# A graph network in one kernel: the third layer's early products run in an even line, their sums stay in the PSUM bank, and ten row slots are kept

## The chip, the cores and the metric

The kernel runs on one core of one Trainium2 chip. The metric is the device time of one execution, in microseconds (us). The kernel before took 2517.03 us (median of three runs, 2515.44 to 2526.33). One further execution was profiled and took 2523.93 us.

## What is computed

A layer norm with ReLU, four graph layers on 6250 nodes and 100000 edges (sorted by destination), a last linear map, and a residual. Cut to what matters:

```python
h = relu(layernorm(x))                                        # 6250 x 256
h = h @ W1_self + mean(h[src] by dst) @ W1_neigh + b1         # layer 1
hp = relu(h @ W2_pool + b2_pool)
h = h @ W2_self + max(hp[src] by dst) @ W2_neigh + b2         # layer 2: max pooling
h = ((sum(h[src] by dst) + h) / (deg + 1)) @ W3_neigh + b3    # layer 3: a sum by dst
h = h @ W4_self + mean(h[src] by dst) @ W4_neigh + b4         # layer 4
return x + h @ W_fc + b_fc
```

## The kernel before, in words

Nodes stand in 49 tiles of 128, and destinations are unevenly spread: the first 23 tiles hold most edges. For these, the sum over edges is a dense product: 128x128 blocks of edge counts (`tab_a`, fp8, built in layers 1 and 2) times the rows of the source tiles. For the other tiles it is done edge by edge.

Only layer 2 and what is run inside it matter here. **The chain of layer 2** is the loop over `at`, 1 to 782. In each turn GpSimd (POOL) gathers 128 rows of 2 KB for 128 edges (L1803) into one half of a row pair `X`, of which six are in flight, and VectorE (DVE) takes running maxima (L1784): three steps for two gathers. SyncE's queue (SP) stores one row of each pair (L1788). POOL can fill a pair again only when DVE and the store are through with it. The edges are cut into six blocks, worked last block first; at a block's end `carry` joins the lanes (PE transposes, L1524, then DVE scans, L1537).

**Node tiles.** When a block is done, the node tiles that end in it can be finished by `done2`, a generator that takes one step for each turn: POOL gathers the totals (`tot`, L1658), PE transposes them and multiplies (`pm_prf`, L1689 to L1695), ScalarE (ACT) takes the high part (L1702), PE subtracts it (L1708), ACT takes the low part (L1711), stores both on its own queue (L1712, L1713) and looks at their size (L1597). At most one tile is begun each 11 turns, and not while a block's end is open; beyond that a straight pace holds: `begun2 < 49 * (at - 112) / 634`.

**Early products.** Layer 3 needs, for each of the 23 dense destination tiles, a sum over all source tiles. For source tiles 8 to 39 this is done inside layer 2, as soon as four tiles are finished (a batch of 4): 23 products of 4 items, 92 items, and 736 items in all eight batches. One item is a pair of matmuls (`dense`: L626 with the low fp16 part, L631 with the high part), 512 columns each. A product accumulates in one of two PSUM banks `pd`. SP loads its edge counts (`ae`, L1752, 14 buffers), ACT widens them to fp32 (`aw`, L1739, 4 buffers). After a product, its sum goes into `acc3[d]` in SBUF (printed as `acc`): the first time by an ACT copy (L1438), after that by a DVE add that reads the bank (L1435, `add3`). The call stands with the last but one item of the next product. From `at` 321 on, each turn issues `ceil(left / 48)` items, `left` being what has been added and not issued.

The rows of finished tiles lie in 11 slots (`row_parts`): 8 in `kept_rows`, 3 in a pool of their own.

**Prologue.** Before layer 1, 17 groups of node tiles are normed. `steps` makes products of weights (`pt_w` L285, `pm_w` L291, put away by ACT at L298), one step a group from group 3 and two in groups 7 to 12. They need `w2pf`, loaded by POOL (L1100). In the same turns PE transposes the edge keys (`pt_e`, L1015) and finds where each row of keys begins (`pa`, L932, L934).

Instructions stand on each engine in the order that a scheduler makes of this code; each engine runs its own in that order.

Of the kernel before, what the change touches and what calls it, by code (L numbers as in the profile page):

```python
# [21 lines left out]
P = 128  # L22
# [67 lines left out]
def fast_path(  # L90
# [164 lines left out]
    at = 0  # L255
# [355 lines left out]
                pass  # L611
        del todo[:]

    def dense(ss, block, rows, F, psd, done, extra=0, wide=False, own=None):

        hold = {}

        def run(s):
            if s == ss[0]:
                hold[0] = bank(psd, "pd", "pd", (2 * F if wide else F + extra,))  # L620
            a = block(s)
            z = rows(s)
            if wide:
                nc.tensor.matmul(hold[0], a[0], z, start=(s == ss[0]), stop=(s == ss[-1]))  # L624
            else:
                nc.tensor.matmul(hold[0][:, : F + extra], a[1], z[1][:, : F + extra],  # L626
                                 start=(s == ss[0]), stop=False)
                if s == own:
                    nc.tensor.matmul(hold[0], ident_b, z[1], start=False, stop=False)
                    nc.tensor.matmul(hold[0], ident_r, z[0], start=False, stop=False)  # L630
                nc.tensor.matmul(hold[0][:, :F], a[0], z[0], start=False, stop=(s == ss[-1]))  # L631
            if s == ss[-1]:
                done(hold[0])

        return [lambda s=s: run(s) for s in ss]
# [129 lines left out]
    with ExitStack() as pro:  # L765
# [666 lines left out]
    def add3(d, v):  # L1432

        if d in begun:
            nc.vector.tensor_add(acc3[d], acc3[d], v)  # L1435
        else:
            begun.add(d)
            nc.scalar.copy(acc3[d], v)  # L1438
# [7 lines left out]
    with tc.tile_pool(name="fl2c", bufs=1) as ck, ExitStack() as late:  # L1446
# [273 lines left out]


        BATCH = 4
        ROWS3 = 2 * BATCH + 3
        ready = []
        early = Hub()
        early_pool, split_pool = [], []
        over = {}
        summed = []

        def take_sums():  # L1730
            while summed:
                add3(*summed.pop(0))

        loaded = []

# [5 lines left out]
        def early_products():  # L1741
            batch = dict(ready)
            ss = sorted(batch)
            ready.clear()
            over.update({s: len(early.work) + H3 * len(ss) for s in ss})
            for d in range(H3):
                got = {}
                loaded.append(got)

                def load(d=d, got=got, i=len(loaded) - 1):  # L1750
                    got[0] = early_pool[0].tile([P, BATCH, P], F8, name="ae", bufs=14)
                    nc.sync.dma_start(got[0][:, : len(ss), :].bitcast(BF16),  # L1752
                                      tab_a[d, :, ss[0] : ss[-1] + 1, :])
                    if i >= 2:
                        widened(loaded[i - 2])

                def rows_at(s, got=got):
                    widened(got)
                    return got[1][:, s - ss[0], :], got[0][:, s - ss[0], :]

                work = dense(ss, rows_at, lambda s: batch[s], FH, psd,
                             lambda v, d=d: summed.append((d, v)), own=d)
# [32 lines left out]
        for b in reversed(range(NB)):  # L1795
# [3 lines left out]
            for s0 in range(0, tb, G2):  # L1799
                X = (xmore if at // G2 % 2 else xpool).tile([P, G2, FH], F32, name="X2")  # L1800
                for k in range(G2):
# [27 lines left out]
                    if at == MADE_AT:  # L1829
                        for _ in steps:  # L1830
                            pass
                        top.close()
                        kept_rows += [span3.tile([P, KEPT, FH], dt, tag=f"kept{i}",
                                                 name=f"kept_rows{i}", bufs=1)
                                      for i, dt in enumerate((F32R, F16))]
                        split_pool.append(
# [100 lines left out]
    with ExitStack() as on:  # L1937
# [44 lines left out]
        with tc.tile_pool(name="fl3", bufs=2) as wk:  # L1982
# [37 lines left out]
                yield 1  # L2020

            late = ((0, 4), (4, KEPT), (EARLY[1], 45), (45, NT))
            Z3 = {s: (kept_rows[0][:, s, :], kept_rows[1][:, s, :]) for s in range(KEPT)}
# [694 lines left out]
```

## Time and profile before

| | |
|---|---|
| median of three runs | 2517.03 us |
| the profiled execution | 2523.93 us, its span 2522.0 us |
| busy: PE, DVE, ACT, POOL | 86%, 80%, 50%, 69% of the span |
| layer 2's gathers | from about 650 to 1806 us |
| the early items | from 1125 us on, 624 begun by 1600 us, 112 after |

The page gives busy time by engine; views of the trace give it by stretch, by group of instructions and by instruction, with what ended the idle time before one (`<-`). A busy PE is not a PE at its peak, since matmuls overlap: the distance between two starts is what one costs. PEclk is the clock that PE was granted, as a share of full speed.

### The profile page before, as it was taken

The page shows a single profiled execution, that of the slowest core. Times are in us where ns is not written, and L with a number is a line of the kernel's source. Part 1 is how long each engine was busy: PE and PEld are TensorE (multiplying, and loading weights), DVE is VectorE, ACT ScalarE, POOL GpSimd, SP SyncE. Part 2 cuts the span into 40 slices and gives each one's busy share as a digit, 9 for nine tenths or more (in the row PEclk, how much of TensorE's full clock was granted, in tenths as well). Part 3 has the DMA queues.
Part 4 walks back from the last instruction along what each step waited for, and adds up shares of the span by engine and source line. Part 5 has one row for each costly group of instructions (what it writes and reads, how often), then busy time and mean ns, then how long its engine had stood idle before and what let it go on. Part 6 is the DMA issues. An engine that isn't in the chain of part 4 may idle for free.

```text
span 2522.0 us, 35297 instructions
## 1 busy us (share of the span) xinstructions
PE 2158.2 (86%) x9402; PEld 1248.5 (50%) x9402; DVE 2010.3 (80%) x5565; ACT 1273.2 (50%) x2569; POOL 1729.6 (69%) x2013
## 2 busy tenths in 40 slices
PE   4699999999795565769999999896389999799997
PEld 2456666776443232334444444343244444477776
DVE  7899987785799898888889999798757777467665
ACT  4888888676488787765323333231112222244443
POOL 5477776667566777676667665677477777477775
PEclk9799999999897787789999999898799999899999
DMA  9677777777899999999999999999799999899997
GB/s 306 198 231 233 223 210 213 216 235 238 294 364 303 341 350 346 323 367 357 334 307 339 342 335 301 299 361 326 258 395 407 407 407 407 319 359 333 335 310 234
DMA packets 381357, 785.68 MB, mean 312 GB/s; under 512 B 56430, under 2 KB 175830, under 8 KB 381116
## 3 DMA queue, kind: packets, MB, share of 16 engines
q0 software_dynamic: 135184, 471.64, 56.0%
q1 hardware_dynamic: 158504, 221.70, 24.4%
q10 hardware_dynamic: 87460, 90.01, 10.7%
q8 instruction: 76, 1.25, 0.2%
q14 instruction: 133, 1.09, 0.1%
HBM read 573.99 MB, written 209.94 MB: 311 GB/s over the span
## 4 chain that ended last, share of the span: by engine, by line
PE 45%; DMA 27%; DVE 14%; issue 5%; ACT 5%; POOL 4%; ACTq 0%; DVEq 0%; POOLq 0%; SPq 0%
DMA X<-rows,srcIf 9%; PE pd L626 8%; PE pd L631 8%; PE pd L624 6%; DMA xq<-acc 5%; PE pm_prf L1695 3%; DVE run L1784 3%; DMA ring<-tab_s,srcE 3%; PE pm_hp L1271 3%; PE pm_prf L1689 2%; DMA rows<-X 2%; PE pm_hp L1265 2%; POOL X L1803 2%; PE pm_prf L1692 2%; PE pg L568 2%
## 5 line engine op out<-in xcount | busy, mean ns | idle before, releaser
L1803 POOL DMA_INDIRECT X<-rows,srcIf x782 | 742.7, 950 | 346.1 <-issue 148.8
L1784 DVE SCALAR_TENSOR_TENSOR run<-run,samef,X 128x512 f32<-128x512 f32 x758 | 572.9, 756 | 31.8 <-DMA X<-rows,srcIf 27.0
L548 POOL DMA_INDIRECT ring<-tab_h,srcT x402 | 389.6, 969 | 177.6 <-issue 39.9
L1912 ACT CAST af<-ac 128x640 fp32r<-128x640 fp8e4 (+2 forms) x299 | 217.2, 734 | 339.3 <-PE pd L624 121.7
L548 POOL DMA_INDIRECT ring<-tab_r,srcE x254 | 255.0, 1004 | 102.8 <-issue 35.1
L1784 DVE SCALAR_TENSOR_TENSOR X<-X,samef,run 128x512 f32<-128x512 f32 x379 | 281.9, 744 | 40.2 <-issue 19.7
L548 POOL DMA_INDIRECT ring<-tab_s,srcE x254 | 244.5, 963 | 93.0 <-issue 23.5
L602 DVE SCALAR_TENSOR_TENSOR acc<-pg,M,acc 128x256 f32<-128x256 f32 (+2 forms) x556 | 281.3, 533 | 31.6 <-PE pg L573 16.3
L573 PE MATMUL pg<-ring,hot 128*128 128x256 f32 (+1 forms) x656 | 292.2, 455 | 0.0
L631 PE MATMUL pd<-kept_rows,aw 128*128 128x512 f32 x529 | 271.0, 588 | 0.0
L1739 ACT CAST aw<-ae 128x512 fp32r<-128x512 fp8e4 x184 | 113.8, 620 | 252.1 <-PE pd L631 225.0
L570 PE MATMUL pg<-ring,hot 128*128 128x259 f16 (+1 forms) x656 | 211.5, 325 | 28.7 <-DMA ring<-tab_r,srcE 8.3
L626 PE MATMUL pd<-kept_rows,ae 128*128 128x512 f16 x529 | 208.5, 394 | 10.7 <-DMA ae<-tab_a 8.4
L1695 PE MATMUL pm_prf<-unf,hTf 128*128 128x512 f32 x384 | 196.9, 637 | 6.1 <-ACT hTf L1685 5.4
L631 PE MATMUL pd<-Z1h,af 128*128 128x256 f32 x588 | 194.8, 364 | 1.0 <-ACT af L1299 1.0
L544 DVE TENSOR_SCALAR hot<-iota_bf,keyE 128x128 fp32r<-128x128 bf16 x508 | 138.3, 300 | 48.2 <-PE pg L573 22.7
L624 PE MATMUL pd<-zt,af 128*128 128x512 f32 x598 | 166.3, 398 | 1.5 <-ACT af L1912 1.5
L626 PEld LDWEIGHTS <-ae 128*128 128x128 fp8e4 x736 | 71.3, 97 | 193.0 <-issue 176.6
L626 PE MATMUL pd<-Z1l,A 128*128 128x259 f16 x588 | 158.5, 280 | 0.0
L573 PEld LDWEIGHTS pg<-ring,hot 128*128 128x128 f32 x656 | 130.7, 199 | 47.7 <-issue 39.1
L624 PE MATMUL pd<-z,af 128*128 128x512 f32 x529 | 149.1, 400 | 2.8 <-ACT af L1912 1.5
L463 ACT ACTIVATE A<-pb 128x392 fp8e4<-128x392 f32 x240 | 116.2, 495 | 69.7 <-PE pb L457 65.7
(439 smaller groups left out, 5027.7 us busy)
## 6 DMA issues: line engine op xcount, KB each, us to landing
rows<-X SPq DMA_DIRECT2D x385, 256.0 KB
rows<-hpf SPq DMA_DIRECT2D x49, 256.0 KB
th<-tab_t ACTq DMA_DIRECT2D x49, 256.0 KB
X<-rows,srcIf POOLq DMA_INDIRECT x782
ae<-tab_a SPq DMA_DIRECT2D x184, 64.0 KB
tab_a<-A ACTq DMA_DIRECT2D x15, 784.0 KB
ac<-tab_a ACTq DMA_DIRECT2D x138, 80.0 KB
tab_t<-th SPq DMA_DIRECT2D x37, 256.0 KB
```

The lines of the kernel that those rows point to most:

```text
L544: nc.vector.tensor_scalar(hot[j], iota_b, keyT[:, j - jb : j - jb + 1], None, op0=ALU.is_equal)
L548: nc.gpsimd.indirect_dma_start(out=ring[:, j % deep, :].bitcast(F32), out_offset=None, in_=table, in_offset=bass.IndirectOffsetOnAxis(ap=s ...
L570: nc.tensor.matmul(pg[:, : F + counts], hot[j].bitcast(BF16)[:, 1::2], X.bitcast(F16)[:, 2 * F : 3 * F + counts], start=(k == 0), stop=False)
L573: mm = nc.tensor.matmul(pg[:, :F], hot[j], X[:, :F], start=False, stop=(k == n - 1))
L602: nc.vector.scalar_tensor_tensor(acc[d], half, m, acc[d], op0=ALU.mult, op1=ALU.add)
L624: nc.tensor.matmul(hold[0], a[0], z, start=(s == ss[0]), stop=(s == ss[-1]))
L626: nc.tensor.matmul(hold[0][:, : F + extra], a[1], z[1][:, : F + extra], start=(s == ss[0]), stop=False)
L631: nc.tensor.matmul(hold[0][:, :F], a[0], z[0], start=False, stop=(s == ss[-1]))
L1695: nc.tensor.matmul(pm, hT[:, c, :], un[:, c, :], start=False, stop=(c == KH - 1))
L1784: nc.vector.scalar_tensor_tensor(put, held, st, row, op0=ALU.mult, op1=ALU.max)
L1803: nc.gpsimd.indirect_dma_start(out=X[:, k, :], out_offset=None, in_=tab_p, in_offset=bass.IndirectOffsetOnAxis(ap=srcI[:, t : t + 1], axis=0),
L1912: nc.scalar.copy(wide[i][:, :n, :], got[i][:, :n, :])
```

## The change

1. The sums stay in PSUM. Before a product that continues a sum, ACT copies `acc3[d]` into the product's bank (`lay`, one product ahead), all its matmuls accumulate onto that, and ACT copies the bank back (`take_sums`). The 161 DVE adds are gone; ACT has 161 copies out and 161 copies in that it did not have. Out and in now stand with the second item of a product.
2. The early items run in a line: by turn `at`, `736 * (at - 320) / 432` items have been issued, as far as they exist.
3. The tiles' pace has four corners: 0 at turn 112, 19 at 318, 37 at 612, 49 at 746.
4. 13 slots for rows, 10 of them in `kept_rows`. A row that takes a slot first issues what is left of the products that read the slot's last row.
5. The prologue's product steps begin at group 4, and groups 7 to 13 take two.

```diff
-FIRST_AT = 112
 EARLY_AT = 310
+SLOTS = (10, 13)
+PACE = ((112, 0), (318, 19), (612, 37), (746, 49))
...
             if s == ss[0]:
-                hold[0] = bank(psd, "pd", "pd", (2 * F if wide else F + extra,))
+                hold[1] = True
+                if begun:
+                    hold[0], hold[1] = begun()
+                else:
+                    hold[0] = bank(psd, "pd", "pd", (2 * F if wide else F + extra,))
...
-                                 start=(s == ss[0]), stop=False)
+                                 start=(s == ss[0] and hold[1]), stop=False, **more)
...
-                for _ in range(2 if 7 <= g < 13 else g >= 3):
+                for _ in range(2 if 7 <= g < 14 else g >= 4):
                     next(steps, None)
...
         def row_parts(d):
-            i = d % ROWS3
-            assert early.done >= over.get(d + ROWS3, 0)
+            i = slot[d]
+            if d in held_by:
+                early.advance(over[held_by[d]])
...
-            if i < KEPT:
+            if i < SLOTS[0]:
...
+        early_all = H3 * (EARLY[1] - EARLY[0])
...
         def take_sums():
             while summed:
-                add3(*summed.pop(0))
+                d, v = summed.pop(0)
+                begun.add(d)
+                nc.scalar.copy(acc3[d], v)
+
+        def lay(i):
+            if i < len(order3) and i not in laid:
+                t = bank(psd, "pd", "pd")
+                d = order3[i]
+                laid[i] = t, d not in begun
+                if d in begun:
+                    nc.scalar.copy(t, acc3[d])
...
-                def then(w):
+                def then(w, i=i):
                     take_sums()
+                    lay(i + 1)
                     w()
 
-                early.add([(load, work[0])] + [lambda w=w, i=i: then(w) if i == len(work) - 2 else w()
-                                               for i, w in enumerate(work[1:])])
+                early.add([(load, work[0]), lambda w=work[1], then=then: then(w), *work[2:]])
...
+        def paced(at):
+            for (a0, n0), (a1, n1) in zip(PACE, PACE[1:]):
+                if at < a1:
+                    break
+            return n0 + (n1 - n0) * (at - a0) / (a1 - a0)
...
-                        early.advance(early.done + math.ceil(
-                            early.left() / max(1, min(48, T - 24 - at))))
+                        early.advance(math.ceil(early_all * (at - EARLY_AT - 10)
+                                                / (T - 40 - EARLY_AT)))
...
-                            and begun2 < NT * (at - FIRST_AT) / (T - 36 - FIRST_AT)):
+                            and begun2 < paced(at)):
```

What moves is shown at three places; line numbers after the change are a few higher. First DVE, in the third batch of early products, before. `X` is a row pair (the number is its buffer), `run` the running maximum, `acc_1` the sum of destination tile 1, `pd` the bank:

```order
L1784 SCALAR_TENSOR_TENSOR run<-run,samef,X_16590 128x512
L1435 TENSOR_TENSOR acc_1_10192<-acc_1_10192,pd 128x512
L1784 SCALAR_TENSOR_TENSOR X_16590<-X_16590,samef,run 128x512
L1784 SCALAR_TENSOR_TENSOR run<-run,samef,X_16590 128x512
L1784 SCALAR_TENSOR_TENSOR run<-run,samef,X_16619 128x512
L1784 SCALAR_TENSOR_TENSOR X_16619<-X_16619,samef,run 128x512
L1784 SCALAR_TENSOR_TENSOR run<-run,samef,X_16619 128x512
L1784 SCALAR_TENSOR_TENSOR run<-run,samef,X_16649 128x512
L1435 TENSOR_TENSOR acc_2_10193<-acc_2_10193,pd 128x512
```

And DVE in the same part of layer 2 now:

```order
L1820 SCALAR_TENSOR_TENSOR run<-run,samef,X_16802 128x512
L1820 SCALAR_TENSOR_TENSOR X_16802<-X_16802,samef,run 128x512
L1820 SCALAR_TENSOR_TENSOR run<-run,samef,X_16802 128x512
L1820 SCALAR_TENSOR_TENSOR run<-run,samef,X_16827 128x512
L1820 SCALAR_TENSOR_TENSOR X_16827<-X_16827,samef,run 128x512
```

Only the running maxima are left on DVE there. Second ACT, in the second batch, before: `aw` is the widened count block, `kept_rows`, `hTf`, `th` and `tab_r` belong to node tiles:

```order
L1685 COPY hTf<-pt_hTf 128x512
L1739 CAST aw<-ae 128x512 x2
L1664 DMA th_15666<-tab_t 128x512
L1739 CAST aw<-ae 128x512
L1702 CAST kept_rows_11380<-pm_prf 128x512
L1712 DMA tab_r<-kept_rows_11380 128x512
L1597 ACTIVATE hTf,zsum<-kept_rows_11380 128x512
L1739 CAST aw<-ae 128x512 x3
```

And now:

```order
L1753 COPY acc_8_10199<-pd 128x512
L1768 CAST aw<-ae 128x512
L1761 COPY pd<-acc_10_10201 128x512
L1710 CAST kept_rows_11380<-pm_prf 128x512
L1720 DMA tab_r<-kept_rows_11380 128x512
L1605 ACTIVATE hTf,zsum<-kept_rows_11380 128x512
L1753 COPY acc_9_10200<-pd 128x512
L1768 CAST aw<-ae 128x512
L1761 COPY pd<-acc_11_10202 128x512
```

For each product ACT empties the last bank (L1753), widens a block, and fills the same bank for the product after the next (L1761); a node tile's copies stand between. Third PE in the prologue, before:

```order
L1015 MATMUL pt_e<-identf,rF 128x128 x5
L285 MATMUL pt_w<-identf,wl 128x128 x4
L291 MATMUL pm_w<-w2pf,wT 128x512 x4
L1015 MATMUL pt_e<-identf,rF 128x128 x5
L932 MATMUL pa<-SN,sel_261 128x2
```

And now:

```order
L1022 MATMUL pt_e<-identf,rF 128x128 x5
L939 MATMUL pa<-SN,sel_261 128x2
L941 LDWEIGHTS later
L941 MATMUL pa<-unit,later 128x2
L939 MATMUL pa<-SN,sel_261 128x2
L941 LDWEIGHTS later
L941 MATMUL pa<-unit,later 128x2
L939 MATMUL pa<-SN,sel_261 128x2
L1022 MATMUL pt_e<-identf,rF 128x128 x5
L286 MATMUL pt_w<-identf,wl 128x128 x4
L292 MATMUL pm_w<-w2pf,wT 128x512 x2
```

The second set of key transposes and the first row starts now stand ahead of the first product with the loaded weights `w2pf`.

More of the change, by code (lines that the diff above doesn't have):

```diff
@@ L612, in sums, with dense @@
         del todo[:]
-    def dense(ss, block, rows, F, psd, done, extra=0, wide=False, own=None):
+    def dense(ss, block, rows, F, psd, done, extra=0, wide=False, own=None, begun=None):
         hold = {}
@@ L625, in run @@
             else:
+                more = {} if hold[1] else {"skip_group_check": True}
                 nc.tensor.matmul(hold[0][:, : F + extra], a[1], z[1][:, : F + extra],
-                                 start=(s == ss[0]), stop=False)
+                                 start=(s == ss[0] and hold[1]), stop=False, **more)
                 if s == own:
-                    nc.tensor.matmul(hold[0], ident_b, z[1], start=False, stop=False)
-                    nc.tensor.matmul(hold[0], ident_r, z[0], start=False, stop=False)
-                nc.tensor.matmul(hold[0][:, :F], a[0], z[0], start=False, stop=(s == ss[-1]))
+                    nc.tensor.matmul(hold[0], ident_b, z[1], start=False, stop=False, **more)
+                    nc.tensor.matmul(hold[0], ident_r, z[0], start=False, stop=False, **more)
+                nc.tensor.matmul(hold[0][:, :F], a[0], z[0], start=False, stop=(s == ss[-1]),
+                                 **more)
             if s == ss[-1]:
@@ L1722, in fast_path @@
         BATCH = 4
-        ROWS3 = 2 * BATCH + 3
+        slot, held_by, last = {}, {}, {}
+        for d in reversed(range(NT)):
+            slot[d] = i = (EARLY[1] - 1 - d) % SLOTS[1] if d >= 4 else 3 - d
+            assert d >= KEPT or i < SLOTS[0]
+            if d < EARLY[1]:
+                if i in last:
+                    held_by[d] = last[i]
+                last[i] = d
+        assert all(d >= EARLY[0] for d in held_by.values())
+        early_all = H3 * (EARLY[1] - EARLY[0])
         ready = []
@@ L1759, in rows_at, with begin @@
                     return got[1][:, s - ss[0], :], got[0][:, s - ss[0], :]
+                i = len(order3)
+                order3.append(d)
+                def begin(i=i):
+                    lay(i)
+                    return laid.pop(i)
                 work = dense(ss, rows_at, lambda s: batch[s], FH, psd,
-                             lambda v, d=d: summed.append((d, v)), own=d)
-                def then(w):
+                             lambda v, d=d: summed.append((d, v)), own=d, begun=begin)
+                def then(w, i=i):
                     take_sums()
+                    lay(i + 1)
                     w()
-                early.add([(load, work[0])] + [lambda w=w, i=i: then(w) if i == len(work) - 2 else w()
-                                               for i, w in enumerate(work[1:])])
+                early.add([(load, work[0]), lambda w=work[1], then=then: then(w), *work[2:]])
         todo = []
@@ L1832, in fast_path @@
                         top.close()
-                        kept_rows += [span3.tile([P, KEPT, FH], dt, tag=f"kept{i}",
+                        kept_rows += [span3.tile([P, SLOTS[0], FH], dt, tag=f"kept{i}",
                                                  name=f"kept_rows{i}", bufs=1)
@@ L2022, in fast_path @@
             late = ((0, 4), (4, KEPT), (EARLY[1], 45), (45, NT))
-            Z3 = {s: (kept_rows[0][:, s, :], kept_rows[1][:, s, :]) for s in range(KEPT)}
+            Z3 = {s: tuple(v[:, slot[s], :] for v in kept_rows) for s in range(KEPT)}
             with tc.issue_after(kept_stores[-1].ins):
```

1 line of the change is left out of this document (added).

## The prediction

> **What bounds the kernel now.** I read the page first, then the table of windows for the stretch in which early products run, then the groups and the waits of its slowest part, then single instructions. POOL leads the chain of layer 2: its last gather is what layer 3 waits for. So the question in each window is how many gathers POOL gets through (its columns come last before PEclk), and who holds it.
>
> ```profile
> span 2522.0 us, 35297 instructions
> core 0: us, PE busy (x) PEld busy (x) DVE busy (x) ACT busy (x) POOL busy (x), PEclk, DMA share, GB/s
> 1103.00:1200.00 97.00, 82.38 (x287) 38.18 (x287) 81.03 (x180) 45.76 (x85) 69.55 (x75) 0.93 1.02 367
> 1200.00:1600.00 400.00, 393.81 (x1476) 191.57 (x1474) 363.81 (x546) 122.41 (x222) 265.42 (x280) 0.99 0.96 324
> 1103.00:1600.00 497.00, 476.18 (x1761) 229.75 (x1761) 444.85 (x725) 168.18 (x306) 334.97 (x354) 0.98 0.97 333
> 1125.00:1600.00 475.00, 458.83 (x1716) 221.57 (x1716) 427.01 (x686) 157.50 (x289) 318.36 (x336) 0.98 0.97 329
> 1600.00:1700.00 100.00, 87.31 (x294) 42.41 (x294) 80.72 (x122) 26.74 (x53) 72.99 (x78) 0.93 0.97 339
> 1600.00:1725.00 125.00, 103.93 (x364) 49.74 (x364) 104.33 (x157) 30.82 (x59) 89.51 (x96) 0.93 0.95 328
> 1725.00:1806.00 81.00, 35.77 (x95) 17.72 (x95) 67.04 (x103) 9.23 (x20) 57.74 (x61) 0.71 0.97 331
> ```
>
> One POOL instruction takes 97 / 75 = 1.29 us from 1103 to 1200, 400 / 280 = 1.43 from 1200 to 1600, and 100 / 78 = 1.28 after that. The slow stretch is where DVE adds sums. Undisturbed, POOL issues one each 1.25 us, 0.95 busy and 0.30 of issue:
>
> ```profile
> 1401.35 0.94 POOL L1803 DMA_INDIRECT X<-rows,srcIf  x1 [0.30 <-issue]
> 1405.10 0.95 POOL L1803 DMA_INDIRECT X<-rows,srcIf  x1 [0.30 <-issue]
> L1803 POOL DMA_INDIRECT X<-rows,srcIf x262 | 248.6, 949 | 127.4 <-issue 49.9 <-DVE run L1784 42.0 <-DVE X L1784 13.5
> L1784 DVE SCALAR_TENSOR_TENSOR run<-run,samef,X 128x512 f32<-128x512 f32 x256 | 193.3, 755 | 3.7 <-DMA X<-rows,srcIf 1.0
> L1784 DVE SCALAR_TENSOR_TENSOR X<-X,samef,run 128x512 f32<-128x512 f32 x128 | 95.3, 745 | 5.2 <-issue 1.6 <-DMA X<-rows,srcIf 1.1
> L1435 DVE TENSOR_TENSOR acc<-acc,pd 128x512 f32<-128x512 f32 x129 | 88.3, 685 | 20.4 <-PE pd L631 18.1 <-ACT kept_rows L1702 0.9
> ```
>
> The first two lines are single gathers (start, duration), the others the groups from 1200 to 1600. DVE is the holder: POOL waits for its steps, and DVE waits for a gathered row only 1.0 + 1.1 us in 400. It is busy 363.81 us, of which the adds are 88.3, and idle 20.4 before the adds: 384 of 400. But PE is busy 393.81 of the same 400. Two bounds lie on each other, and the change takes away one of them.
>
> **The change part by part.** The sum is made against the profiled execution, 2523.93 us (span 2522.0 and 1.9 around it), which is 6.9 above the median of 2517.03; the difference found is then taken from the median.
>
> *The adds leave DVE.* From 1200 to 1600, 88.3 + 20.4 = 109 us go from DVE, which then needs 364 - 88 = 276 of 400. Late next is POOL itself. From 1103 to 1600 it has 354 instructions: 354 x 1.25 = 442 us at its own pace, 354 x 1.29 = 457 at the pace it has on either side. I take 1.29, since carries at block ends and waits for stores stay: 497 - 457 = **-40 us**. The lower end is 442 (-55).
>
> *Can PE follow?* From 1125, where early items begin, PE is busy 458.8 us. One item is one pair, 0.46 us:
>
> ```profile
> 1407.86 0.39 PE L626 MATMUL pd<-kept_rows,ae 128*128 128x512 f16 x1
> 1408.32 0.39 PE L626 MATMUL pd<-kept_rows,ae 128*128 128x512 f16 x1
> 1100.00:1600.00 500.00, 244.63 (x624) 60.34 (x624) 0.98 0.97 333
> 1600.00:1806.00 206.00, 44.47 (x112) 11.01 (x112) 0.85 0.96 329
> 1403.37 1.88 PE L1695 MATMUL pm_prf<-unf,hTf 128*128 128x512 f32 x4
> ```
>
> (The third and fourth lines count items, the fifth is a quarter of a node tile's products: next start 1.72 later, so 7 us a tile, about 8 with transposes.) The old rule, worked through the loop, has issued 607 items by gather 643, the last one before 1600; the line 736 x 323 / 432 = 550. That is 57 x 0.46 = 26 us less. The new pace, with its 11 turns between tiles and block ends, has begun 17 tiles by turn 320 and not 16: 8 us less. PE needs 459 - 26 - 8 = 425 us, and has 457 - 22 (from 1103 to 1125) = 435. It fits, with 10 us to spare. The tile that comes earlier lies where PE has room, 37 busy of 50, so it costs nothing there:
>
> ```profile
> 1050.00:1100.00 50.00, 37.42 (x116) 16.82 (x117) 43.63 (x112) 40.56 (x97) 36.04 (x39) 0.86 0.98 344
> ```
>
> If that room were gone, it would cost its 8 us.
>
> *Fills and empties on ACT.* ACT was busy 122 of 400 us. It gets about 114 products' copies out and in before 1600 (550 / 4 less the first 23). No row shows ACT writing a bank from SBUF; the nearest are a bank read to SBUF and an SBUF pass:
>
> ```profile
> L1438 ACT COPY acc<-pd 128x512 f32<-128x512 f32 x23 | 13.5, 586 | 21.5 <-PE pd L631 21.4
> L1597 ACT ACTIVATE hTf<-r2h 128x512 f32<-128x512 f32 x9 | 5.7, 630 | 1.4 <-DMA ae<-tab_a 1.0 <-ACT r2h L1702 0.4
> L1739 ACT CAST aw<-ae 128x512 fp32r<-128x512 fp8e4 x131 | 81.1, 619 | 195.9 <-PE pd L631 175.6 <-DMA rows<-X 10.1 <-DMA ae<-tab_a 5.0
> ```
>
> I take 0.6 us. ACT's 114 x 1.2 = 137 us fit beside its 122. What is new is a chain: a bank's last matmul, copy out 0.59, a widening 0.62 that stands between, copy in 0.6, then the first matmul of the product after the next. That is 1.8 us and the hand-overs, and PE meanwhile has one product, 4 x 0.46 = 1.84. Where products follow back to back, PE waits 0 to 0.3 us each; where a node tile's matmuls lie between, nothing. Queued behind a late copy are the node tiles' copies on ACT, and PE waits for those too. Half of 0.3 for 114 products is 17 us, 10 of which are PE's room: **+8 us** (0 to +35, the upper end with 0.4 us at each). What longer waits do shows in one place, where PE once waited for a late add:
>
> ```profile
> 1198.43 0.38 PE L626 MATMUL pd<-r2l,ae 128*128 128x512 f16 x1 [2.73 <-DVE acc L1435]
> 1199.57 0.60 PE L626 MATMUL pd<-kept_rows,ae 128*128 128x512 f16 x1
> 1200.39 0.65 PE L626 MATMUL pd<-kept_rows,ae 128*128 128x512 f16 x1
> ```
>
> After 2.73 us of waiting, pairs are 0.82 apart instead of 0.46. The row shows it for a wait of that length alone, and I expect shorter ones. The Trainium skill (TensorE: Matmul & The Clock Gate, A second HAM failure mode: psum-queue depth-cycling) says that short idle times between groups of matmuls that cycle through PSUM banks are enough to swing the clock between half and full. By that rule the sum would be the second rival's below. PEclk of 0.98 from 1125 to 1600, with products cycling through two banks, does not bear it out so far.
>
> *The end of layer 2.* The line has 186 items left at gather 643, not 129: 26 us more for PE after 1600. There PE idles 125 - 104 = 21 us up to 1725 and 45 after. But node tiles come at their densest, and a carry makes DVE wait for PE's transposes. I charge half: **+13 us** (0 to +26).
>
> *The prologue.* PE's queue stood still for a load, with the key transposes behind it:
>
> ```profile
> 33.47 6.46 PE L291 MATMUL pm_w<-w2pf,wT 128*128 128x512 f32 x8 [11.01 <-DMA w2pf<-in_L_gnn_W_pool]
> 40.40 0.89 DVE L1019 CAST srcT<-pt_e 128x512 int32<-128x512 f32 x2 [3.16 <-PE pt_e L1015]
> 39.96 0.60 ACT L298 ACTIVATE Wa<-pm_w 128x512 f32<-128x512 f32 x1 [11.47 <-PE pm_w L291]
> 34.75 0.43 DVE L808 BATCH_NORM_STATS2 st<-xt 128x6 f32<-128x256 f32 x1 [5.05 <-DMA xt<-in_x]
> ```
>
> The transposes now go first, and DVE's 3.16 us go: **-3 us** (-6 to +1; DVE's other wait, for `xt`, stays, and the products end a group later).
>
> *The slots* add no instruction. A tile that takes a slot 13 tiles on finds its products issued: tile 26 takes tile 39's at about turn 383, when the line stands at 107 and the batch ends at 92. Cost nothing; a burst of items on PE if the line lagged.
>
> Sum: -40 + 8 + 13 - 3 = **-22 us**, 2501.9 for the profiled execution and **2495** for the median.
>
> **The rivals.**
> *PE stays the bound.* If each fill costs 0.4 us, PE needs 425 + 46 = 471 us from 1125, and the stretch 493 instead of 497. With +5 to +13 at the end and -3: 2517 - 4 + 9 - 3 = 2519. For it: PE at 393.81 of 400. Against: 34 us of its work go elsewhere.
> *Waits for fills lower PE's clock (slower).* Place: the first matmul of each continued product. At a PEclk of 0.86, as in the row of 1050 to 1100, 425 us become 494, the stretch 516: +19, +13 at the end, -3: 2546. It decides for slower once the mean clock there falls below 425 / 475 = 0.89. Against: PE is given work without gaps. The skill's rule above speaks for it.
> *Transfers set the pace.* DMA share is 0.96 where gathers are slow. Then the stretch gains some 8 us and the rest adds up to 2517. Against: 367 GB/s at 1.29 us a gather, and DVE that waits for rows 2 us in 400.
> *Nothing holds POOL any more.* 1.25 us throughout, fills hidden, no charge at the end: 2517 - 55 - 4 = 2458.
> *The change doesn't even anything out.* The order of the program shows the adds gone and the copies there, so only the line's effect could be missing; that is the first rival.
>
> **How the numbers follow.** The forecast gets 0.50, POOL alone 0.10, PE as bound 0.20, transfers 0.08, the lower clock 0.12. A difference of 0.5% is 12.6 us, about what a measurement of this kernel can tell from no change. The forecast with its own uncertainty (-22, its terms -55 to +1 at their ends) is mostly beyond that: faster 0.48 + 0.10 = 0.58; same 0.02 + 0.20 + 0.08 = 0.30; slower 0.12. The range, 2466 to 2526, leaves out the lower clock and half of the lowest case.
>
> **What would show it.** Right: from the first early item on, POOL at 1.28 to 1.31 us an instruction, waiting for `issue` and not for DVE; DVE 75 to 80% busy; 345 ACT copies between `acc` and `pd` (184 out, 161 in) at 0.6; PE waiting for ACT at `pd` under 20 us in sum and PEclk at 0.97 or more; the last gather some 20 us earlier; layer 1's first gather 3 us earlier. Wrong: PE waiting for the copy in at most products, PEclk under 0.9, or POOL still at 1.4 with DVE idle.

## The result, and the profile after

The changed kernel takes 2510.06 us (median of six runs, 2508.67 to 2512.47); the kernel before, in six runs beside them, 2525.15 us (2515.44 to 2528.47). The ratio is 0.9948, 95% interval 0.9931 to 0.9965: faster by 13 us, where 22 were forecast (the medians lie 15 us apart, and the six runs of the kernel before spread over 13). The profiled execution took 2510.62 us, its span 2508.7.

First the table of windows of the changed kernel, for the stretch and for the end of layer 2 (columns as before: PE, PEld, DVE, ACT, POOL with instructions, then PEclk, DMA share, GB/s):

```profile
span 2508.7 us, 35344 instructions
1103.00:1200.00 97.00, 89.62 (x320) 43.38 (x318) 78.45 (x167) 45.61 (x88) 68.90 (x74) 0.96 1.02 362
1200.00:1600.00 400.00, 355.11 (x1303) 173.21 (x1301) 317.94 (x458) 221.74 (x434) 290.07 (x306) 0.96 0.99 344
1103.00:1600.00 497.00, 444.73 (x1621) 216.59 (x1619) 396.39 (x625) 267.34 (x521) 358.97 (x379) 0.96 0.99 347
1600.00:1755.00 155.00, 130.10 (x455) 64.71 (x455) 112.66 (x166) 72.40 (x143) 110.02 (x117) 0.92 0.96 331
1755.00:1815.00 60.00, 55.24 (x181) 27.72 (x180) 15.34 (x43) 21.09 (x43) 5.67 (x7) 0.96 0.42 132
```

From 1200 to 1600 POOL now makes 306 instructions and not 280: 400 / 306 = 1.31 us each. DVE is busy 79% of that time, no longer 91. The new row is the last: for 60 us POOL is busy 6, DVE 15 and the transfers 0.42 of the time, while PE is busy 55. The groups of the same 400 us say who waits for whom (busy, mean ns, then the idle time ahead and its releasers):

```profile
L1845 POOL DMA_INDIRECT X<-rows,srcIf x289 | 274.7, 951 | 105.1 <-issue 63.8 <-DVE run L1820 20.6 <-DVE X L1820 12.9
L1820 DVE SCALAR_TENSOR_TENSOR run<-run,samef,X 128x512 f32<-128x512 f32 x281 | 212.4, 756 | 28.5 <-DMA X<-rows,srcIf 24.4
L1761 ACT COPY pd<-acc 128x512 f32<-128x512 f32 x117 | 69.5, 594 | 36.8 <-DMA ae<-tab_a 18.3 <-DMA rows<-X 18.1 <-ACT acc L1753 0.4
L1753 ACT COPY acc<-pd 128x512 f32<-128x512 f32 x117 | 68.6, 586 | 105.1 <-PE pd L637 77.7 <-DMA ae<-tab_a 18.3 <-DMA rows<-X 4.2
```

A copy in takes 0.594 us, as I took it. But the copies stand behind transfers (`ae<-tab_a`, `rows<-X`) for some 60 of these 400 us, and a copy between `acc` and `pd` needs no transfer. The waits of PE from 1200 us to the end of layer 2 show what that does (us in total, times, longest):

```profile
PE pd L632 <- ACT pd L1761: 42.7, 19, 6.1
PE pcf L1569 <- DVE cTf L1548: 12.2, 1, 12.2
PE pt_hTf L1690 <- DVE tot L1686: 6.6, 1, 6.6
PE pm_prf L1697 <- DVE segf L1544: 5.6, 1, 5.6
```

Where the 13 us come from is read from POOL. The windows that count its gathers stand in two fences, of before and of after; then its last gather of layer 2 and its first of layer 3, again of before and of after:

```profile
600.00:1102.60 502.60, 296.02 (x312) 0.84 0.94 326
600.00:1599.30 999.30, 609.88 (x643) 0.91 0.96 329
600.00:1802.40 1202.40, 741.85 (x782) 0.90 0.96 329
```

```profile
600.00:1089.90 489.90, 297.19 (x312) 0.85 0.95 333
600.00:1552.50 952.50, 611.65 (x643) 0.90 0.97 341
600.00:1755.10 1155.10, 743.19 (x782) 0.90 0.97 339
```

```profile
1802.31 0.94 POOL L1803 DMA_INDIRECT X<-rows,srcIf  x1 [0.30 <-issue]
1827.02 0.94 POOL L548 DMA_INDIRECT ring<-tab_r,srcE  x1 [13.61 <-DVE oddI L78]
```

```profile
1755.04 0.95 POOL L1845 DMA_INDIRECT X<-rows,srcIf  x1 [0.30 <-issue]
1813.74 0.94 POOL L549 DMA_INDIRECT ring<-tab_r,srcE  x1 [33.05 <-DVE oddI L79]
```

The same starts, read in the same way from the four experiments below that ran beside a kernel before of 2520 us (us; in brackets the difference to before):

| stretch | before | after | adds on DVE | old rule | transfers on SP | three banks |
|---|---|---|---|---|---|---|
| start to gather 312 | 1102.6 | 1089.9 (-12.7) | 1087.5 (-15.1) | 1092.2 (-10.3) | 1097.6 (-4.9) | 1095.3 (-7.2) |
| gather 312 to 643 | 496.7 | 462.5 (-34.2) | 498.5 (+1.8) | 464.2 (-32.4) | 450.7 (-46.0) | 459.2 (-37.5) |
| gather 643 to 782 | 203.1 | 202.6 (-0.5) | 205.4 (+2.3) | 210.8 (+7.7) | 200.5 (-2.5) | 210.1 (+7.0) |
| gather 782 to layer 3's first | 24.7 | 58.7 (+34.0) | 24.5 (-0.2) | 57.7 (+33.0) | 39.5 (+14.8) | 63.4 (+38.7) |
| layer 3's first to the end | 695.0 | 695.0 (0) | 695.0 (0) | 695.2 (+0.2) | 696.0 (+1.0) | 694.6 (-0.4) |

So the stretch gained its 34 us, and the end of layer 2 gave the same 34 us back. The 13 us that are left stem from ahead of gather 312, where no early item has run yet.

Where PE stood shows what the end pays for. The count in brackets is of early items begun in the changed kernel, first up to gather 643, then up to the last gather:

```profile
1100.00:1552.40 452.40, 195.49 (x491) 0.96 0.99 350
1100.00:1755.10 655.10, 284.47 (x711) 0.95 0.98 344
```

By gather 643 the line has issued 550 items, and PE has begun 491 of them; in the kernel before it had begun 624. At the last gather 25 of the 736 items are still to come; before had begun them all.

### The profile page after: what moved, and what is told of

It reads as the page before. It is cut to its first block, busy times and chain, and to the rows that moved or that the text cites. A ratio compares the mean times of both kernels' runs of the same rounds, so it can differ in the third digit from the quotient of the medians.

```text
span 2508.7 us, 35344 instructions
## 1 busy us (share of the span) xinstructions
PE 2155.9 (86%) x9402; PEld 1254.0 (50%) x9402; DVE 1916.4 (76%) x5404; ACT 1427.3 (57%) x2891; POOL 1728.7 (69%) x2013
## 3 DMA queue, kind: packets, MB, share of 16 engines
q1 hardware_dynamic: 158504, 221.70, 24.4%
## 5 line engine op out<-in xcount | busy, mean ns | idle before, releaser
L637 PE MATMUL pd<-kept_rows,aw 128*128 128x512 f32 x598 | 315.2, 601 | 0.0
L632 PE MATMUL pd<-kept_rows,ae 128*128 128x512 f16 x598 | 240.2, 402 | 42.5 <-ACT pd L1761 32.3
L571 PE MATMUL pg<-ring,hot 128*128 128x259 f16 (+1 forms) x656 | 211.7, 326 | 37.5 <-DMA ring<-tab_h,srcT 15.6
L1753 ACT COPY acc<-pd 128x512 f32<-128x512 f32 x184 | 107.8, 586 | 205.0 <-PE pd L637 147.1
L637 PEld LDWEIGHTS pd<-kept_rows,aw 128*128 128x128 f32 x598 | 123.6, 207 | 70.9 <-issue 69.0
```

The costliest lines, as they stand in the source:

```text
L571: nc.tensor.matmul(pg[:, : F + counts], hot[j].bitcast(BF16)[:, 1::2], X.bitcast(F16)[:, 2 * F : 3 * F + counts], start=(k == 0), stop=False)
```

## The experiments

The theory after the result (A): the adds on DVE did hold the gathers, but the copies in and out stand in ACT's queue behind its own transfers; PE waits for them, falls back, and layer 3 waits for PE. The rivals: (B) the 57 items that the line moves past gather 643 are what the end pays; (C) PE's sheer work sets the end, wherever it lies.

**Adds on DVE.** Everything as changed, but the sums are added on DVE.

```diff
-                begun.add(d)
-                nc.scalar.copy(acc3[d], v)
+                add3(d, v)
...
-                    lay(i)
-                    return laid.pop(i)
+                    return bank(psd, "pd", "pd"), True
...
-                    lay(i + 1)
```

> The changed kernel with the sums added on DVE again, as before (161 adds of 0.68 us); the line, the slots and the prologue stay as changed. Theory A (the adds on DVE held POOL's gathers, and taking them away is what let the last gather come 47 us earlier): POOL back at about 1.4 us an instruction from 1200 to 1600, last gather at 1795 to 1810, time 2515 to 2530. Rival (the even line or the prologue made the gain): POOL near 1.28, time 2505 to 2513.

Measured: 2510.87 us beside 2519.91, ratio 0.995 (0.9934 to 0.9967). The table of windows and the groups of 1200 to 1600:

```profile
1200.00:1600.00 400.00, 380.28 (x1429) 185.10 (x1428) 355.80 (x540) 116.86 (x210) 263.96 (x280) 0.97 0.95 321
```

```profile
L1442 DVE TENSOR_TENSOR acc<-acc,pd 128x512 f32<-128x512 f32 x130 | 88.7, 682 | 22.7 <-PE pd L637 22.3
```

POOL is back at 400 / 280 = 1.43 us, so the adds do hold the gathers: that part of A holds. But the time is the rival's, and the last gather, at 1791.3, lies outside A's 1795 to 1810. Both are true, since the stretch's 34 us and the 34 us of the end go together: without the sums in PSUM the kernel has neither. All of this kernel's 11 us lie ahead of gather 312 (-15.1); the line with adds on DVE adds nothing.

**The old rule** for the items, in place of the line.

```diff
-                        early.advance(math.ceil(early_all * (at - EARLY_AT - 10)
-                                                / (T - 40 - EARLY_AT)))
+                        early.advance(early.done + math.ceil(
+                            early.left() / max(1, min(48, T - 24 - at))))
```

> The changed kernel with the old rule for when items are issued (what is left over 48 turns) in place of the line. Theory A (PE's fill waits and its whole work set the end of layer 2, not the place of the items): 57 items more before gather 643, as many fewer after; PE's backlog at the last gather is much the same; time within 8 us of 2510. Rival B (the 57 late items, 26 us, are what the end of layer 2 pays): layer 3 starts 15 to 26 us earlier, time 2484 to 2495.

Measured: 2515.58 us, ratio 0.9977 (0.9962 to 0.9991). The profiled run gives back 33.0 us after the last gather, as many as with the line, and PE waits 32.8 us for fills. The items that it has begun by its last gather, and these waits:

```profile
1100.00:1767.30 667.30, 285.81 (x709) 0.93 0.98 339
PE pd L632 <- ACT pd L1761: 32.8, 12, 6.8
```

The old rule issues items earlier, but PE has begun 709 by the last gather, against 711 with the line. Rival B falls: the late items are not what the end pays.

**Transfers on SP.** A finished tile's load of `th` and its two stores to `tab_r` are issued by SP.

```diff
-            nc.scalar.dma_start(th, tab_t[d].rearrange("p (k n) -> p k n", n=P))
+            nc.sync.dma_start(th, tab_t[d].rearrange("p (k n) -> p k n", n=P))
...
-            nc.scalar.dma_start(tab_r[d * P : (d + 1) * P, :FH], hi.bitcast(F32))
-            nc.scalar.dma_start(tab_r[d * P : (d + 1) * P, FH:], lo.bitcast(F32))
+            nc.sync.dma_start(tab_r[d * P : (d + 1) * P, :FH], hi.bitcast(F32))
+            nc.sync.dma_start(tab_r[d * P : (d + 1) * P, FH:], lo.bitcast(F32))
```

> The changed kernel with the node tiles' three transfers (the load of th, the two stores to tab_r) issued by SP and not by ACT. Theory A (ACT stands 2 to 7 us at each of these issues until an earlier transfer has landed, the fills queue behind, and PE waits 43 us for them): PE's waits at pd for ACT fall below 15 us, the last gather stays near 1755, layer 3 starts 20 to 30 us earlier, time 2480 to 2490. Rival B or C (late items, or PE's sheer work, set the end): waits may fall, but the time stays within 6 us of 2510. Against both: SP stands at these issues instead, row stores come late, and POOL slows: over 2515.

Measured: 2486.28 us, ratio 0.9856 (0.9829 to 0.9883). To see why, one long wait of the changed kernel, first on ACT (ACTq is its sequencer, issuing a transfer), then on PE, then on SP's queue:

```profile
1732.11 0.58 ACT L1710 CAST kept_rows<-pm_prf 128x512 fp32r<-128x512 f32 x1
1739.36 0.33 ACTq L1720 DMA_DIRECT2D tab_r<-kept_rows  x1
1739.73 0.63 ACT L1605 ACTIVATE hTf<-kept_rows 128x512 f32<-128x512 f32 x1 [7.04 <-DMA rows<-X]
...
1740.36 0.57 ACT L1753 COPY acc<-pd 128x512 f32<-128x512 f32 x1
1740.83 0.62 ACT L1768 CAST aw<-ae 128x512 fp32r<-128x512 fp8e4 x1
1741.35 0.59 ACT L1761 COPY pd<-acc 128x512 f32<-128x512 f32 x1
```

```profile
1741.99 0.58 PE L632 MATMUL pd<-kept_rows,ae 128*128 128x512 f16 x1 [6.05 <-ACT pd L1761]
1742.80 0.65 PE L632 MATMUL pd<-kept_rows,ae 128*128 128x512 f16 x1
1743.68 0.65 PE L632 MATMUL pd<-kept_rows,ae 128*128 128x512 f16 x1
```

```profile
1728.36 12.04 SPq L1824 DMA_DIRECT2D rows<-X  x5
```

ACT has the row ready at 1732.69 and issues its store at 1739.36. The copy out, a widening and the copy in all come after it, and PE stands for 6.05 us. The list of instructions shows what ACT waits for. The scheduler of this program gives each transfer of SP and of ACT one of eight landing counters (`DMAHW0` to `DMAHW7`), which a transfer raises when it has landed; the two engines take them in turn, and each transfer first waits for the counter's last one. The first six rows are SP's, from a stretch of its list that is cut at the dots; the numbers go up by one, but skip 4, 0 and 6. These are the numbers of ACT's next three transfers (the last three rows):

```
L1824 DMA rows_72<-X_17467 128x512 [waits DMAHW3_49,DVE_49]
L1824 DMA rows_72<-X_17493 128x512 [waits DMAHW5_49,DVE_49]
...
L1824 DMA rows_72<-X_17518 128x512 [waits DMAHW7_49,DVE_49]
L1781 DMA ae<-tab_a 128x256 [waits DMAHW1_49,PE_49,Activation_49]
...
L1781 DMA ae<-tab_a 128x256 [waits DMAHW5_49,PE_49,Activation_49]
L1781 DMA ae<-tab_a 128x256 [waits DMAHW7_49,PE_49,Activation_49]

L1672 DMA th_17631<-tab_t 128x512 [waits DMAHW4_49,PE_49]
L1720 DMA tab_r<-kept_rows_11380 128x512 [waits DMAHW0_49,Activation_49]
L1721 DMA tab_r<-kept_rows_11381 128x256 [waits DMAHW6_49,Activation_49]
```

By this list ACT cannot issue before the transfer that had the counter last, eight places back and mostly SP's, has landed; and SP's queue stood with row stores that come as DVE delivers them, five in 12 us from 1728 on. So PE was tied to the gathers again, by way of SP's stores and ACT. With the transfers on SP, the waits of ACT's copies in and out over all of layer 2, and the end of the gathers:

```profile
L1761 ACT COPY pd<-acc x161: 582/593/623, 1179.9 to 1752.2; 128x512 f32<-128x512 f32 x161
its engine sat idle before it (us, times) until:
  PE pd L637: 230.0, 132
who waited for it (us, times):
  PE pd L632: 0.5, 1
```

```profile
1748.88 0.95 POOL L1845 DMA_INDIRECT X<-rows,srcIf  x1 [0.30 <-issue]
...
1788.37 0.94 POOL L549 DMA_INDIRECT ring<-tab_r,srcE  x1 [21.88 <-DVE odd L76]
```

No copy waits for a landing any more, PE's waits for fills go from 42.7 to 0.5 us, and the two spans differ by 24.3 us: 19.2 after the last gather, 11.8 in the stretch and 2.1 behind it, with 7.8 lost ahead of gather 312 and 1.0 in layer 3 and 4. At the last gather PE has begun 726 items:

```profile
1100.00:1748.90 648.90, 286.62 (x726) 0.94 0.99 349
```

A is shown on this chip, for 19 of the 34 us at the end. The Trainium skill (DMA: Bandwidth & Descriptors, Rules for kernel authors) says that spreading transfers over SP, ACT and GpSimd gives no bandwidth and only saves the issuing sequencer's time. The trace agrees: the DMA share from 1200 to 1600 is 0.99 in both kernels, and what was won is the time that ACT stands at its issues. By C nothing should have changed, so it falls as the whole cause. What the 14.8 us are that the end still costs is not shown. PE stands 63 us from 1200 us on in four waits for DVE at block ends (20.7 for `tot`, 22.6 for `X`, 19.9 for `segf`), which the forecast's sum of PE's busy time does not hold.

**Three banks** for the products, fills two products ahead.

```diff
-name="pst2", bufs=3
+name="pst2", bufs=2
...
-name="psd2", bufs=2
+name="psd2", bufs=3
...
-                    lay(i + 1)
+                    lay(i + 2)
```

> The changed kernel with three banks for the early products (one less for the node tiles' transposes and products, 2 and not 3) and the fill laid two products ahead. Theory A: each wait for a fill is shorter by one product, 1.84 us, so 43 us become 15 to 25; layer 3 starts 12 to 22 us earlier, time 2488 to 2498, if the node tiles do not miss their bank. Rival B or C: within 6 us of 2510.

Measured: 2526.4 us, ratio 1.0026 (1.0006 to 1.0046). A miss: PE's waits for fills fall only to 35.6 us. One product more of slack, 1.84 us, does not cover a wait of 6 us. PE also waits 26.0 us at `pt_hTf` for DVE's `tot` and 14.2 for `segf`; but the old rule and the transfers on SP, with all their banks, wait 24.4 and 20.7 us for `tot`, so the bank taken from the node tiles is not shown to be the reason. Why this kernel is slower than the changed one stays open.

**On five other chips.** The later runs fell on chips on which the kernel before takes 2933 to 2973 us, with the same instructions. From 95 to 600 us, ahead of all that the change touches in layer 2, PE makes 2505 matmuls of the changed kernel on one of these chips, and 3040 in its first profile. What was measured (medians in us):

| kernel | this | before | ratio (95%) |
|---|---|---|---|
| adds on DVE, transfers on SP | 2952.38 | 2932.85 | 1.0066 (1.0028 to 1.0103) |
| the same, second | 2963.32 | 2935.59 | 1.0073 (1.0034 to 1.0112) |
| the same, third | 2982.94 | 2964.6 | 1.0049 (1.0017 to 1.0081) |
| the same, fourth | 2988.53 | 2972.96 | 1.0033 (1.0005 to 1.0061) |
| before, new prologue | 2936.07 | 2932.85 | 1.0009 (0.9984 to 1.0033) |
| before, new pace | 2934.28 | 2932.85 | 1.0011 (0.9986 to 1.0035) |
| before, new prologue and pace | 2941.25 | 2935.59 | 1.0022 (0.9995 to 1.0049) |
| the same, second | 2968.95 | 2964.6 | 1.0028 (0.9996 to 1.006) |
| the same, third | 2961.26 | 2972.96 | 0.9973 (0.9936 to 1.0009) |
| transfers on SP, old rule | 2975.34 | 2932.85 | 1.0144 (1.0102 to 1.0186) |
| the same, second | 2972.12 | 2935.59 | 1.0114 (1.0063 to 1.0166) |
| transfers on SP, steeper line | 2980.4 | 2935.59 | 1.0161 (1.0118 to 1.0205) |
| the changed kernel itself | 2996.04 | 2972.96 | 1.0092 (1.006 to 1.0125) |
| transfers on SP | 3014.35 | 2962.58 | 1.016 (1.0117 to 1.0203) |

Their edits are the ones above, put together, and three more: the prologue's steps alone, the tiles' pace alone, and a steeper line.

```diff
-                for _ in range(2 if 7 <= g < 13 else g >= 3):
+                for _ in range(2 if 7 <= g < 14 else g >= 4):
...
-                            and begun2 < NT * (at - FIRST_AT) / (T - 36 - FIRST_AT)):
+                            and begun2 < paced(at)):
...
-                                                / (T - 40 - EARLY_AT)))
+                                                / (T - 80 - EARLY_AT)))
```

Adds on DVE with transfers on SP, four times:

> The changed kernel with the sums added on DVE again and, besides, the node tiles' three transfers issued by SP. Theory A (the transfers on ACT cost only because the copies in and out of the sums queue behind them there): with the adds on DVE nothing on PE's path queues on ACT, so no gain over the adds on DVE alone, 0.995 of before: 0.990 to 0.998. Rival (issuing the transfers from SP is a gain of its own, whatever holds the sums): 0.983 to 0.988, as with the sums in PSUM.

> The kernel of the adds on DVE with the node tiles' transfers on SP, once more, because its first run fell on a chip on which the kernel before takes 2933 us and transfers set the pace. Theory A (the transfers on ACT cost only because copies in and out of the sums queue behind them): 0.990 to 0.998 of before. Rival (issuing from SP is a gain of its own, whatever holds the sums): 0.983 to 0.988.

> Adds on DVE, the line, and the node tiles' transfers on SP, for a chip on which the kernel before takes about 2520 us. Theory A (the transfers on ACT cost only because copies of the sums queue behind them): 0.990 to 0.998 of before, as with these transfers on ACT (0.995). Rival (issuing from SP is a gain of its own): 0.983 to 0.988. Should the chip be one of those at 2930 us: near 1.007, and it tells neither.

> Adds on DVE, the line, the node tiles' transfers on SP. Where before takes 2520 us. Theory A (the transfers on ACT cost only because copies of the sums queue behind them): 0.990 to 0.998. Rival (issuing from SP is a gain of its own): 0.983 to 0.988. On a chip at 2930 us: 1.004 to 1.008, as in three such runs.

Prologue, pace, and both together:

> The kernel before with the new steps of the prologue alone. My term was -3 (-6 to +1). Layer 1's first gather came at 93.37 before and at 91.54 and 90.79 in two runs of the new steps, layer 2's first at 653.03, 652.67 and 649.67. Theory A: 1 to 4 us earlier at layer 2's first gather, 312 to 315 gathers by 1103, 0.9985 of before (0.997 to 1.000). Rival (the prologue makes the 9 gathers, 12 us, that the changed kernel has ahead at 1103): 319 to 323 gathers by 1103, 0.995.

> The kernel before with the new pace of the node tiles alone (PACE in place of one straight line). I charged it nothing. Theory A: gathers by 1103 within 3 of 312, and 0.998 to 1.002 of before. Rival (the pace makes the 9 gathers, 12 us, that the changed kernel has ahead at 1103, before any early item runs): 318 or more gathers by 1103, 0.994 to 0.997.

> The kernel before with the prologue's new steps and the node tiles' new pace, nothing else. Theory (these two make what the changed kernel has ahead at 1103, 4 to 11 gathers; the line and the sums, as they stand, bring nothing): 316 to 323 gathers by 1103, 0.994 to 0.998 of before, as with the adds on DVE and the line. Rival (they make 3 us or less, and the line the rest): 311 to 315 gathers, 0.998 to 1.001.

> The kernel before with the prologue's new steps and the node tiles' new pace, for a chip on which the kernel before takes about 2520 us. Theory (these two make what the changed kernel gained; line and sums net nothing): 316 to 323 gathers by 1103, 0.994 to 0.998 of before. Rival (they make 3 us or less): 311 to 315 gathers, 0.998 to 1.001. On a chip at 2930 us: 1.000 to 1.004.

> The kernel before with the prologue's new steps and the node tiles' new pace. Where before takes 2520 us. Theory (these two make what the changed kernel gained): 316 to 323 gathers by 1103, 0.994 to 0.998. Rival (3 us or less): 311 to 315 gathers, 0.998 to 1.001. On a chip at 2930 us: 1.000 to 1.004, as in two such runs.

Transfers on SP with other lines:

> The changed kernel with the node tiles' transfers on SP and the old rule for the items. With the transfers on ACT the old rule was 5 us slower than the line. Theory A (once no fill waits, PE's backlog at the last gather decides; it has 34 us of room from 1500 to 1600 that the line leaves empty): 57 items go there, PE's work after the last gather shrinks by up to 26 us, time 5 to 20 us under the line with transfers on SP: 0.978 to 0.984 of before. Rival (the line is better in itself): 0.986 to 0.990.

> Sums in PSUM, the transfers on SP and the old rule for the items, once more for the same reason. Theory A (without fill waits PE's backlog at the last gather decides, and 57 items can go into the 34 us that PE is idle from 1500 to 1600): 0.978 to 0.984 of before, the time from the last gather to layer 3's first near 25 us and not 39.5. Rival (the line is better in itself): 0.986 to 0.990.

> Sums in PSUM, the transfers on SP, and the line steeper: all items by turn 702 instead of 742 (432 turns become 392), so 56 items more before gather 643, and the last batch of 92 goes in one piece when it is ready. Theory A: between the line and the old rule, 0.980 to 0.986 of before. Rival (PE's sheer work from 1200 on sets the end, wherever the items lie): 0.984 to 0.988, as with the line.

The changed kernel itself, and with transfers on SP:

> The changed kernel itself. Where the kernel before takes about 2520 us: 0.993 to 0.997 of before, as measured. Where it takes about 2930 us because engines stand for reasons outside the program: if the gain rests on gathers that run ahead by 4 to 11 at turn 312 and on nothing else, 0.998 to 1.003; if the fills behind ACT's transfers cost more there, since each landing comes later, 1.003 to 1.015.

> The changed kernel with the node tiles' transfers on SP, again. Where before takes 2520 us: 0.983 to 0.989 of before, PE's waits at pd for ACT under 5 us. Where it takes 2930 to 2970 us, the changed kernel was 1.009 of before with PE waiting 99 us for fills, since ACT itself stands there for reasons outside the program, up to 17 us at a time. Theory (a chain PE, ACT, PE takes in ACT's stalls, and moving the transfers takes only a part of them away): 1.003 to 1.012 and still over 50 us of waits at pd. Rival (the transfers are the larger part there too): under 1.000 and less than 40 us.

What these runs show: prologue and pace make no difference there, alone or together, and no kernel with moved transfers is faster than before. The changed kernel itself is slower there. Its waits in layer 2 (from 1250 us on), first PE's and then ACT's; in the third fence PE's in the kernel before with prologue and pace changed, on the same chip:

```profile
PE pd L632 <- ACT pd L1761: 99.2, 18, 11.7
PE pd L632 <- issue: 45.0, 11, 7.8
```

```profile
ACT acc L1753 <- remote: 178.0, 23, 17.1
ACT acc L1753 <- PE pd L637: 101.4, 51, 6.5
```

```profile
PE ptcf L1524 <- DVE X L1784: 46.7, 2, 28.6
PE pd L626 <- DVE acc L1435: 39.0, 16, 8.4
```

ACT stands 178 us for something that the profile does not name ("remote"), up to 17 us at a time, and the sums in PSUM carry that to PE: 99 us of waits for fills against 39 for DVE's adds. I expected that moving the transfers would leave 1.003 to 1.012; it was 1.016, with 86.3 us of waits for fills, so most of ACT's waits are others there. What they are was not found; nor is it shown that transfers set the pace there, as one of the expectations has it. These runs leave two questions open for a chip like that of the first four experiments: whether the transfers on SP help with adds on DVE, and whether prologue and pace make what lies ahead of gather 312.

## Why the prediction was wrong, and what in it was right

The step that failed is *Fills and empties on ACT*. It priced a fill by the three ACT instructions of its chain, at 0 to 0.3 us a product, and put what stands ahead of them in ACT's queue at nothing. There 19 fills stood behind ACT's own transfers, and PE waited 42.7 us for them. With this step fell "It fits, with 10 us to spare", and the bill came in the term for the end of layer 2, which measured +33.5 us and not +13. The prologue's term, -12.7 and not -3, hid 10 us of that.

- **The adds leave DVE, with fills on ACT: -40 and +8 in the stretch.** Right: 497 us should have become 465 and became 462.5. POOL takes 1.31 us (forecast 1.28 to 1.31), DVE is busy 79% (75 to 80), and the copies are 184 out and 161 in, of 0.59 us.
- **Can PE follow?** "It fits, with 10 us to spare" was wrong. PE idles 45 of 400 us from 1200 on, 33 of them for fills. At gather 643 it is 59 items behind the line. At the last gather it has begun 711 of 736 items and the last matmul of 44 of 48 tiles; before had begun all items by then, and that of 47 tiles.
- **The fills' price.** I asked how long copy out, widening and copy in take, found 1.8 us against 1.84, and put 0 to 0.3 us on each product. That chain is as fast as I said: of 161 fills, 142 cost nothing that the waits show. But 19 cost 42.7 us, since I had looked at what stands behind a late copy on ACT, and not at what the copies stand behind: ACT's own transfers. (Half of 0.3 us for 114 products, less 10, is 7 us; the sum has 8.)
- **The end of layer 2: +13.** This is the mis-sized term: it measured +33.5 (-0.5 to the last gather, +34.0 after it), beyond its upper end of 26. Its reason was wrong too. The late items cost nothing there (the old rule gives the same 33 us); PE's arrears do. The transfers on SP take 19 of the 34 away; the rest is open.
- **The prologue: -3.** Layer 1's first gather came at 91.54 and not 93.37, layer 2's first at 652.67 and not 653.03. So some 2 us are there at first, and 0.4 at layer 2. But gather 312 starts 12.7 us earlier. Half of that, 6.6 us, is there at gather 112, and up to turn 112 neither pace begins a tile, so the code differs only in the prologue; another 5.5 us come between gathers 250 and 280. Three of the kernels have the same code up to gather 312 (this one, adds on DVE, the old rule). They start it 10.3 to 15.1 us earlier than the one profile of before, so a part of it is how executions differ; the rest I could not place.
- **Sum.** Terms of -40, +8, +13 and -3 measured -34.2 (the first two), +33.5 and -12.7. The direction came out right for a wrong reason: what I took for the gain came to nothing, and the 13 us lie ahead of it, where I expected 3. That is luck.
- **The signs.** POOL's pace, DVE's share and the copies came as named. PE's waits for ACT (42.7 us, not under 20) and PEclk (0.96 from 1103 to 1600, not 0.97 or more) did not, and the last gather came 47 us earlier, not some 20.
- **The lower clock** did not decide: PEclk of 0.96 is not below 0.89.
- **PE stays the bound** was the rival nearest to the truth. It put the bill for the fill waits into the stretch, which it saw at 493 us; the stretch took 462.5, and the bill came after the last gather.

## What to carry to other kernels

When a copy on an engine becomes part of another engine's chain, read what stands ahead of it in that engine's queue, its transfers and their waits above all, and not only what the copy itself takes. When an engine that paced two others is relieved, ask which of the two is in arrears at the end of the stage: the faster chain then stands and waits for the other. A gain in a stretch counts only after the hand-over behind it.

## What the runs showed of the hardware

- How long PE must stand before its clock falls. In the changed kernel's stretch, fill waits of 0.45 to 2.32 us were followed by pairs 0.46 us apart, and so was one of 3.06; after waits of 3.46, 4.28, 4.38, 5.19 and 6.05 us the pairs were 0.81 to 0.88 apart for 3 to 6 us, as in the rows at 1742. Length alone does not decide: the 2.73 us of the prediction's row were followed by slow pairs too, and so was a wait of 2.70 us for a landing, at 1713.63. The Trainium skill (TensorE: Matmul & The Clock Gate, What's actually happening) has the clock fall after an idle window of some 3.4 us that runs freely. The trace agrees for the waits of 3.46 us and more; the two of 2.7 us are shorter than that window, so here it need not be idle throughout. The Trainium skill's rule on short idle times, which the prediction weighed, was not seen.
- The kernel before took 2520 to 2525 us where the change was first measured and beside the first four experiments, and 2933 to 2973 on five other chips. The change's sign went with it: 0.9948 (0.9931 to 0.9965) where it was first measured, 1.0092 (1.006 to 1.0125) on one of the five.
- Before, after and the kernel with adds on DVE all take 695.0 us from layer 3's first gather to the end, so what was won or lost ahead of it reached the end undiminished.
